# Three of 32 blocks, not four, are left out of the grouped expert pass

## The chip, the core and the metric

One Trainium2 chip, one of its cores. The time is that of one execution on the device in microseconds; a version's time is the median over its runs. The engines are TensorE (PE: matmuls, with weight loads beside them), VectorE (DVE), ScalarE (ACT), GpSimd (POOL) and SyncE (SP). Each works off its own queue of instructions in order. SP, ACT and POOL also issue transfers (DMA): SP and ACT plain ones, POOL here the indirect ones, whose row numbers come from a table on the chip. Everything is in fp32.

## The reference

Two layers on an image batch x of shape (4, 256, 64, 64). The first is a 3x3 neighbourhood attention behind a group normalisation; the second works on the 4 x 4096 tokens of 256 channels and ends with a mixture of 8 experts, of which each token uses 2:

```python
x = x + conv_attn(_gn(x))                  # 3x3 local attention, Wq, Wk, Wv, Wo
t = _to_tokens(x)                          # (4, 4096, 256)
t = t + windowed_gate(_ln_t(t))            # tanh projection, sigmoid gate, sums over 64 tokens
t = t + moe(_ln_t(t))
x = _from_tokens(t, x)

def moe(tokens):
    tokens = layer-normed t
    rw, re = top_k(softmax(tokens @ router_w.T), 2)    # rw scaled to sum 1
    out = tokens
    for e in range(8):
        h = gelu(tokens @ w1[e] + b1[e], approximate=False)
        out = out + combine[:, e:e+1] * (h @ w2[e] + b2[e])
    return out
```

## The kernel before

The 16384 tokens are worked in 32 blocks (`NB`) of 512 (`TB`), 8 blocks an image. For a block the functions `produce`, `attend`, `tail` and `ranks` run as generators, interleaved by the main loop (L1482): in turn g the block g is in `attend`, g - 1 in `tail`, g - 2 in `ranks`, g + 1 in `produce`. A scheduler then sets each engine's order from the program order and its own estimates.

*Tokens to experts.* `tail` ends with a block's normed tokens in `tok` (256 channels, 8 weights, 8 words with the place to which a result belongs). `ranks` counts, for each of the 1024 choices of a block, the row in the expert's region of the HBM array `rows_in`, and `give` (L1001) scatters the block with 8 indirect transfers on POOL, 128 rows each, one for each of 4 tiles and 2 choices. They wait in the list `waiting` and are let out a few at a time.

*Groups and slots.* Blocks are put in groups. When a group's last block is counted, a small plan is made on DVE (L1041 to L1112): how many full units of 256 rows (`UP`) each expert has by now, and so which expert and which rows each *slot* of the group has. A slot is 256 rows of one expert. A group of two blocks has 8 slots, one of one block 4; the first group has 7 fewer, so that there are always enough full units. `experts` runs a slot in stages: `fetch` (SP, L1171), `matrix` (ACT copies the expert's first matrix, L1188), `pixels` (PE transposes L1195, ACT copy L1199), `hidden` (PE L1207, ACT Gelu L1213), `output` (PE L1225, DVE L1229 and L1230) and `add` (L1244): two indirect transfers on POOL that add the results to `out`. The adds of one slot wait for those of the slot before to land, since two slots can hold one token's two choices. `follow` (L1466) says how many slots are due at each point of the main loop: between a limit `most`, which keeps them behind the groups' plans, and a straight line `wanted`, which ends 11, 7 and 3 slots before the last at turns NB, NB + 1 and NB + 2.

*Blocks apart.* The last four blocks (28 to 31, from `NS` on) are in no group. Their rows, with what is left of the groups' rows below a full unit (at most `LEFT` = 21 pieces), are worked at the end by `halves`, in `HALVES` = 2 * 4 * 512 / 128 + 21 = 53 *halves* of 128 rows: fetch (L1319), ACT copy of the matrix (L1331), transposes (L1334), products (L1344, Gelu L1350, L1360), DVE (L1364 to L1372). A half's result is scattered to `sums_a` by POOL (L1373), one row for each token and choice, so nothing has to be added there. The 21 left-over pieces are also added to `out` by L1390 for tokens of earlier blocks, each behind the add before. Each half gives a credit of 1, each such add, and each of the last three slots' adds, costs 2; what is owed at the last half is let out then.

*The end.* The tokens of the blocks apart stay in SBUF: `held` (L875) of blocks 28 and 29 in the pool `xsp`, those of 30 and 31 in their own tile `x1`. `together` (L1421) loads both choices' sums of a block from `sums_a` in two transfers of 512 KB, one on SP and one on ACT, adds them on DVE (L1448) and stores the block. The tiles for these loads take the place of other tiles: blocks 28 and 29 of the pool `xpp`, block 30 of the pool `w2p` (tag "wx"), block 31 of the pool `w3p` (tag "xl_tok"), whose three buffers the left-over pieces use before, four in each.

The lines that set groups and slots:

```python
NS = NB - 4
GROUPS = (*[2] * 13, *[1] * 2)
slots_of = [2 * n * TB // UP for n in GROUPS]
slots_of[0] -= E - 1
HALVES = 2 * (NB - NS) * TB // P + LEFT
```

They give 8 x 13 - 7 + 4 x 2 = 105 slots.

Of the kernel before, what the change touches and what calls it, by code (L numbers as in the profile page):

```python
# [46 lines left out]
FP = mybir.dt.float32  # L47
# [5 lines left out]
P = 128  # L53
# [9 lines left out]
def hybrid_block_kernel(ctx: ExitStack, tc: tile.TileContext, ins: dict, out: bass.AP):  # L63
    nc = tc.nc
    x = ins["x"]
    B, C, FW, _ = x.shape
# [4 lines left out]
    NT = TB // P  # L71
    NBI = HW // TB
    NB = B * NBI
    E = ins["w1b"].shape[0]
# [15 lines left out]
    FETCH = 2  # L90
    I32, U32 = mybir.dt.int32, mybir.dt.uint32
    ENG = mybir.EngineType
    NS = NB - 4
    GROUPS = (*[2] * 13, *[1] * 2)
    assert sum(GROUPS) == NS
    first_of = [sum(GROUPS[:k]) for k in range(len(GROUPS))]
    where = [(k, j) for k, n in enumerate((*GROUPS, NB - NS)) for j in range(n)]
    APART = len(GROUPS)

    U = 2  # L100
    UP = U * P
    slots_of = [2 * n * TB // UP for n in GROUPS]
    slots_of[0] -= E - 1
    assert slots_of[0] > 0
    first_slot = [sum(slots_of[:k]) for k in range(len(GROUPS) + 1)]
    LEFT = U * (E - 1) + E - 1
    HALVES = 2 * (NB - NS) * TB // P + LEFT
    SLOTS = max(*slots_of, HALVES)
# [3 lines left out]
    OWN = SPARE + HALVES * P  # L112
    ROOM_S = 2 * (NB - NS) * TB

# [9 lines left out]
    w2p = ctx.enter_context(tc.tile_pool(name="w2p", bufs=2))  # L124
# [137 lines left out]
    for d in range(2):  # L262
# [4 lines left out]
        part = near[:, d].rearrange("p a b -> p (a b)")  # L267
# [10 lines left out]
    for n in range(2):  # L278
        t = const.tile([P, NG, HALF], FP, tag=f"pe_{n}", name=f"pe_{n}")
# [41 lines left out]
    def iota(name, shape, pattern, base=0, by_partition=0):  # L321
        t = const.tile(shape, FP, tag=name, name=name)
        nc.gpsimd.iota(
            t, pattern=pattern, base=base, channel_multiplier=by_partition,
            allow_small_or_imprecise_dtypes=True,
        )
        return t
# [5 lines left out]
    place_a = iota(  # L333
        "place_a", [P, NB - NS, NT], [[2 * TB, NB - NS], [2 * P, NT]], base=OWN, by_partition=2
    )
# [84 lines left out]
    both = range(NC)  # L420
# [326 lines left out]
    def store(g, t, first=0):  # L747
        at = g * TB + first * P
        inst = nc.sync.dma_start(
            out[at : at + t.shape[1] * P, :].rearrange("(t p) c -> p t c", p=P), t  # L750
        ).ins
        tc.declare_no_dep(inst, group="adds", reason="sums of other blocks' rows")
        tc.add_to_no_dep_group("stores", inst)
        stored.append(inst)

    def tail(g):
# [18 lines left out]
        for pair in range(0, NT, 2):  # L775
            ps = ps_a.tile([P, 2, A + E], FP, tag="a", name=f"psp_{g}_{pair}")
            for u in range(2):
                t = pair + u
# [5 lines left out]
            for u in range(2):  # L784
                t = pair + u
# [13 lines left out]
        wx = w2p.tile([P, NT, C + 1 + E], FP, tag="wx", name=f"wx_{g}")  # L799
# [50 lines left out]
        for pair in range(0, NT, 2):  # L850
            ps = ps_a.tile([P, 2, C], FP, tag="a", name=f"psw_{g}_{pair}")
            window(ps, (slice(None), slice(pair, pair + 2), slice(0, C)))
            for u in range(2):
                t = pair + u
# [16 lines left out]
        if g < RAMP:  # L871
            scales()
        sent = t2
        if NS <= g < NS + 2:
            sent = xsp.tile([P, NC, TB], FP, tag="xs", name=f"held_{g}")  # L875
            sent = sent.rearrange("p c n -> p (c n)").rearrange("p (t c) -> p t c", t=NT)
        at = tc.cur_priority
# [543 lines left out]
    def together():  # L1421

        part = NT // 2
        for g in range(NS, NB):
            sums_of = None
            for n in range(0, NT, part):
                if g == NB - 1:
                    both = w3p.tile([P, NT, RW], FP, tag="xl_tok", name=f"both_{g}_{n}")
                    both = both.rearrange("p t r -> p (t r)")[:, 0 : 2 * part * C]
                    both = both.rearrange("p (t k c) -> p t k c", k=2, c=C)  # L1430
                elif g == NB - 2:
                    both = w2p.tile([P, NT, C + 1 + E], FP, tag="wx", name=f"both_{g}_{n}")
                    both = both.rearrange("p t r -> p (t r)")[:, 0 : 2 * part * C]
                    both = both.rearrange("p (t k c) -> p t k c", k=2, c=C)
                else:
                    if n == 0:
                        sums_of = xpp.tile([P, NT, 2, C], FP, tag="xp", name=f"both_{g}")
                    both = sums_of[:, n : n + part]
                first = OWN + 2 * ((g - NS) * TB + n * P)
                (nc.scalar if n else nc.sync).dma_start(  # L1440
                    both,
                    sums_a[first : first + 2 * part * P, :].rearrange(
                        "(t p k) c -> p t k c", p=P, k=2
                    ),
                )
                own = held[g][:, n : n + part]
                for k in range(2):
                    nc.vector.tensor_add(own, own, both[:, :, k, :])  # L1448
                store(g, own, n)
# [32 lines left out]
    for g in range(NB + 2):  # L1482
        for n in range(*stats_at[g]):
            channel_stats(n)
        if g + 1 < NB:
            for n in range(*stats_at[g + 1]):
                load_xs(n)
        gens = [attend(g), ranks(g - 2), tail(g - 1), produce(g + 1)]
        if g + 3 < NB and (g + 3) % NBI == 0:
            gens.append(image_norm((g + 3) // NBI))  # L1490
        if g == 2:
            load_experts()
        n = 0
        while gens:
            for gen in list(gens):
                if next(gen, gens) is gens:
                    gens.remove(gen)
                    continue
                n += 1
                follow(g + min(n / STEPS.get(g, 27), 0.999))  # L1500
# [6 lines left out]
    for rest in (stream, units):  # L1507
        for _ in rest:
            pass
    together()  # L1510


# [56 lines left out]
```

## Time and profile before

| | us |
|---|---|
| median of 9 runs | 1217.36 |
| lowest, highest | 1214.28, 1220.08 |
| the profiled execution | 1214.2 |
| its span in the profile | 1212.5 |

| lines | work | count | busy us | mean ns |
|---|---|---|---|---|
| L1207, L1225, L1195 (PE) | a slot's products and transposes | 840, 840, 420 | 204.9, 213.2, 65.2 | 385, 385, 278 |
| L1244 (POOL) | adds of slots to `out` | 210 | 335.3 | 1596 |
| L1001 (POOL) | scatters of tokens to `rows_in` | 256 | 256.3 | 1001 |
| L1229, L1230 (DVE) | a slot's bias and weight | 210, 210 | 87.5, 76.6 | 417, 365 |
| L1373 (POOL) | scatters of halves to `sums_a` | 53 | | 957 to 1087 |
| L1390 (POOL) | adds of left-over pieces to `out` | 21 | | 1589 to 1619 |

A row of the groups' table names line, engine and operation, with the sum of the durations and their mean. A matmul in fp32 shows as two records, so 840 records of L1207 are 4 matmuls in each of 105 slots. The order of the stages is seen from the first and last starts: L1244 runs from 188.9 to 1083.7 us, L1001 from 84.7 to 1037.6, L1373 from 1066.2 to 1189.9, L1390 from 1088.3 to 1182.9, and the additions of `together` from 1197.5 on. The clock granted to PE over the span is 0.976 of full speed.

### The profile page before, as it was taken

How to read it: one execution, taken by the hardware profiler on the slowest of the kernel's cores; microseconds unless marked ns; L12 is line 12 of the kernel's file. 1: busy time of each engine (PE TensorE's matmuls, PEld its weight loads, DVE VectorE, ACT ScalarE, POOL GpSimd, SP SyncE). 2: the span in 40 equal slices, each digit the busy share in tenths (PEclk: the TensorE clock that was granted, in tenths of full speed). 3: DMA queues.
4: the chain of work that ended last, by engine and by line, in shares of the span. 5: the costliest groups of instructions: out<-in, count | busy, mean ns of one | idle time of the engine just before them, and what ended most of it. 6: DMA issues, size and time to landing. Idle time of an engine off the chain costs nothing. (4 is left out here: it accounts for less than half of the span.)

```text
span 1212.5 us, 29026 instructions
## 1 busy us (share of the span) xinstructions
PE 1108.1 (91%) x8762; PEld 791.5 (65%) x8762; DVE 916.0 (76%) x4632; ACT 856.2 (71%) x1752; POOL 703.9 (58%) x642
## 2 busy tenths in 40 slices
PE   5989889999999999999999999999999999868890
PEld 4545456677776667766677766766776677757780
DVE  4588878888888888887888887888878888324444
ACT  1466769788888788777787787877787766436660
POOL 3114226566664666576665756566565768577772
PEclk9999999999999999999999999999999999979996
DMA  9895547776768677778786767667665446745556
GB/s 283 267 308 177 175 138 238 209 173 169 186 177 173 160 222 178 187 200 215 164 166 166 192 171 179 168 172 173 141 171 128 101 103 135 177 88 122 144 124 238
DMA packets 136145, 214.00 MB, mean 176 GB/s; under 512 B 16368, under 2 KB 102400, under 8 KB 131768
## 3 DMA queue, kind: packets, MB, share of 16 engines
q1 hardware_dynamic: 86264, 137.00, 37.1%
q0 software_dynamic: 48352, 73.05, 30.3%
q10 hardware_dynamic: 1376, 2.10, 0.5%
q8 instruction: 73, 1.20, 0.4%
q14 instruction: 80, 0.66, 0.2%
HBM read 120.78 MB, written 91.31 MB: 175 GB/s over the span
## 5 line engine op out<-in xcount | busy, mean ns | idle before, releaser
L1244 POOL DMA_INDIRECT out<-sx x210 | 335.3, 1596 | 202.8 <-issue 32.2
L1001 POOL DMA_INDIRECT rows_in<-tok,rows x256 | 256.3, 1001 | 195.4 <-issue 72.5
L1225 PE MATMUL psy<-w,h 128*128 x840 | 213.2, 385 | 1.2 <-DVE qbb L525 0.7
L1207 PE MATMUL psh<-xc,w1s 128*128 128x256 f32 x840 | 204.9, 385 | 0.3 <-ACT h L1213 0.3
L1225 PEld LDWEIGHTS psy<-w,h 128*128 128x128 f32 x840 | 152.7, 190 | 51.6 <-issue 24.9
L1207 PEld LDWEIGHTS psh<-xc,w1s 128*128 128x128 f32 x840 | 152.5, 191 | 35.3 <-issue 10.0
L576 PE MATMUL psq<-x,qks 128*128 128x512 f32 x256 | 125.5, 612 | 1.8 <-ACT qks L497 1.8
L734 PE MATMUL pso<-mixT,vo 128*128 128x512 f32 x256 | 123.5, 605 | 0.0
L1229 DVE TENSOR_TENSOR sx<-psy,b2b 128x256 f32<-128x256 f32 x210 | 87.5, 417 | 44.8 <-PE psy L1225 36.6
L1213 ACT ACTIVATE h<-psh,w1s 128x256 f32<-128x256 f32 x210 | 88.2, 471 | 31.1 <-PE psh L1207 30.2
L1199 ACT COPY xc<-ptx 128x512 f32<-128x512 f32 x105 | 61.2, 583 | 25.4 <-PE ptx L1195 24.9
L1230 DVE TENSOR_SCALAR sx<-sx 128x256 f32<-128x256 f32 x210 | 76.6, 365 | 2.0
L893 ACT ACTIVATE x<-x,scale 128x256 f32<-128x256 f32 x120 | 63.2, 591 | 18.8 <-DVE scale L867 15.4
L1213 ACT ACT_TABLE_LOAD x59 | 75.7, 1283 | 0.8
L584 ACT ACTIVATE q<-psq,qbb,irc 128x512 f32<-128x512 f32 x64 | 50.0, 781 | 34.5 <-PE psq L576 28.1
L1195 PE MATMUL ptx<-ident,sx 128*128 128x128 f32 x420 | 65.2, 278 | 6.8 <-DMA sx<-rows_in 6.8
L1195 PEld LDWEIGHTS ptx<-ident,sx 128*128 128x128 f32 x420 | 50.6, 144 | 31.4 <-issue 16.3
L780 PE MATMUL psp<-wpr,x1c 128*128 128x136 f32 x512 | 70.2, 282 | 0.5 <-DVE ispread L473 0.5
L576 PEld LDWEIGHTS psq<-x,qks 128*128 128x128 f32 x256 | 46.2, 195 | 35.5 <-issue 34.5
L780 PEld LDWEIGHTS psp<-wpr,x1c 128*128 128x128 f32 x512 | 65.5, 190 | 4.7 <-issue 2.1
L734 PEld LDWEIGHTS pso<-mixT,vo 128*128 128x128 f32 x256 | 45.5, 190 | 34.3 <-issue 30.1
L832 PE MATMUL psw<-wl,bandl 128*64 128x512 f32 x128 | 67.0, 635 | 0.0
(277 smaller groups left out, 2498.6 us busy)
## 6 DMA issues: line engine op xcount, KB each, us to landing
xp<-in_xp SPq DMA_DIRECT2D x32, 1024.0 KB
sx<-rows_in SPq DMA_DIRECT2D x105, 272.0 KB
x<-in_x SPq DMA_DIRECT2D x32, 660.0 KB
xs<-in_xs SPq DMA_DIRECT2D x32, 512.0 KB
out<-x SPq DMA_DIRECT2D x28, 512.0 KB
sxa<-rows_in SPq DMA_DIRECT2D x32, 136.0 KB
rows_in<-tok,rows POOLq DMA_INDIRECT x256
out<-sx POOLq DMA_INDIRECT x210
```

The costliest lines, as they stand in the source:

```text
L576: inst = nc.tensor.matmul(ps.rearrange("p (r w) -> p r w", w=W), qks[:, ci, co * P : (co + 1) * P], t[:, ci, 1 : TH + 1, 1 : W + 1], start ...
L734: nc.tensor.matmul(ps, vo[:, ci, co * P : (co + 1) * P], mixT[:, ci, :], start=(ci == 0), stop=(ci == NC - 1),)
L780: nc.tensor.matmul(ps[:, u, :], xc[:, ci, t * P : (t + 1) * P], wpr[:, ci, :], start=(ci == 0), stop=(ci == NC - 1),)
L832: one = nc.tensor.matmul(to[0:WIN], bandl, wl[part], start=True, stop=True)
L1001: return nc.gpsimd.indirect_dma_start(out=rows_in[:, :], out_offset=bass.IndirectOffsetOnAxis(ap=rows[:, c, t : t + 1], axis=0), in_=tok[: ...
L1195: nc.tensor.transpose(pt[:, c, t * P : (t + 1) * P], xs[:, t, c * P : (c + 1) * P], ident)
L1207: nc.tensor.matmul(ps[:, f, :], w1s[:, o : o + P], xc[:, ci, :], start=(ci == 0), stop=(ci == NC - 1),)
L1213: inst = nc.scalar.activation(h[:, f, :], ps[:, f, :], AF.Gelu, bias=w1s[:, F1 + f : F1 + f + 1])
L1225: nc.tensor.matmul(ps, h[:, f, t * P : (t + 1) * P], w2[:, e, f, :], start=(f == 0), stop=(f == NC - 1),)
L1229: nc.vector.tensor_add(ys[:, t, :], ps, b2b[:, e, :])
L1230: nc.vector.tensor_scalar_mul(ys[:, t, :], ys[:, t, :], xs[:, t, bass.ds(e + C, 1)])
L1244: inst = nc.gpsimd.indirect_dma_start(out=out, out_offset=bass.IndirectOffsetOnAxis(ap=xs[:, t, C + E : C + E + 1].bitcast(U32), axis=0), ...
```

## The change

Block 28 becomes a group of its own, the sixteenth, with four slots; three blocks stay apart. So there are 109 slots and 45 halves where there were 105 and 53. Only block 29 is held in `xsp`, blocks 30 and 31 in their own tiles; block 28 is stored by `tail` and gets its experts' results by adds to `out`. `together` loads the sums of blocks 29 and 30 into the pool `xpp`, those of block 31 into `w3p` as before; the branch for `w2p` goes.

```diff
-    NS = NB - 4
-    GROUPS = (*[2] * 13, *[1] * 2)
+    NS = NB - 3
+    GROUPS = (*[2] * 13, *[1] * 3)
...
-        if NS <= g < NS + 2:
+        if g == NS:
             sent = xsp.tile([P, NC, TB], FP, tag="xs", name=f"held_{g}")
...
                 if g == NB - 1:
                     both = w3p.tile([P, NT, RW], FP, tag="xl_tok", name=f"both_{g}_{n}")
-                    both = both.rearrange("p t r -> p (t r)")[:, 0 : 2 * part * C]
-                    both = both.rearrange("p (t k c) -> p t k c", k=2, c=C)
-                elif g == NB - 2:
-                    both = w2p.tile([P, NT, C + 1 + E], FP, tag="wx", name=f"both_{g}_{n}")
                     both = both.rearrange("p t r -> p (t r)")[:, 0 : 2 * part * C]
                     both = both.rearrange("p (t k c) -> p t k c", k=2, c=C)
                 else:
```

## The prediction

> **What bounds the kernel now.** I read the page first, then busy time by stretch of the span, then the timelines of TensorE (PE), GpSimd (POOL) and VectorE (DVE). A row of the stretch table has its length, then busy time and number of instructions of PE, weight load, DVE, ACT and POOL, then PE's granted clock, DMA share and GB/s.
>
> ```profile
> PE 1108.1 (91%) x8762; PEld 791.5 (65%) x8762; DVE 916.0 (76%) x4632; ACT 856.2 (71%) x1752; POOL 703.9 (58%) x642
> ...
> 250.00:417.00 167.00, 165.91 (x1333) 119.33 (x1331) 140.60 (x725) 138.03 (x260) 100.57 (x85) 1.00 0.72 171
> 417.20:956.10 538.90, 533.88 (x4319) 374.87 (x4317) 451.19 (x2359) 422.42 (x826) 346.38 (x285) 1.00 0.71 173
> 956.00:1043.00 87.00, 79.48 (x437) 64.05 (x434) 71.49 (x336) 53.20 (x103) 62.26 (x50) 0.98 0.57 127
> 1043.00:1066.00 23.00, 15.29 (x96) 13.65 (x96) 4.00 (x14) 11.20 (x29) 9.30 (x6) 0.86 0.78 171
> 1066.00:1192.00 126.00, 99.52 (x646) 85.87 (x646) 49.99 (x166) 70.47 (x181) 94.92 (x80) 0.95 0.51 118
> 1192.00:1212.50 20.50, 0.00 (x0) 0.00 (x0) 9.99 (x16) 0.00 (x0) 0.00 (x0) 0.50 0.86 307
> ```
>
> The reader is to see three regimes. From 250 to 956 PE is busy over 99% at full clock: it sets the time. From 1066 to 1192 (the 128-row halves) PE has 26 us to spare. From 1192 on only transfers and 16 additions are left. The busy sum of the first regime might hide gaps, so I looked at starts:
>
> ```profile
> 625.98 1.89 PE L1207 MATMUL psh<-xc,w1s 128*128 128x256 f32 x8
> 627.71 1.03 PE L1225 MATMUL psy<-w,h 128*128 x4
> 628.66 0.65 PE L618 MATMUL pss<-x,q 128*32 128x60 f32 x32
> 629.24 1.98 PE L734 MATMUL pso<-mixT,vo 128*128 128x512 f32 x4
> 631.06 1.03 PE L1225 MATMUL psy<-w,h 128*128 x4
> 631.93 0.60 PE L1195 MATMUL ptx<-ident,sx 128*128 128x128 f32 x4
> 632.36 1.89 PE L1207 MATMUL psh<-xc,w1s 128*128 128x256 f32 x8
> ```
>
> Each group starts where the one before lets it in, with no idle time noted. From start to next start, a slot's parts here take 0.95 + 0.87 (L1225), 0.43 (L1195) and 1.73 (L1207). In the second regime look at POOL:
>
> ```profile
> 1178.42 1.59 POOL L1390 DMA_INDIRECT out<-sxl,token  x1 [0.44 <-issue]
> 1180.32 0.98 POOL L1373 DMA_INDIRECT sums_a<-sxa,to  x1 [0.30 <-DVE sxa L1371]
> 1181.60 0.96 POOL L1373 DMA_INDIRECT sums_a<-sxa,to  x1 [0.30 <-issue]
> 1182.86 1.60 POOL L1390 DMA_INDIRECT out<-sxl,token  x1 [0.30 <-issue]
> ...
> 1189.91 0.96 POOL L1373 DMA_INDIRECT sums_a<-sxa,to  x1 [0.30 <-issue]
> ```
>
> Between two of its instructions lie 0.30 us whatever is named as releaser, so a scatter (L1373) takes 1.28 and an add (L1390, L1244) 1.90. From the first scatter at 1066.17 to the end of the last at 1190.87 are 124.7 us: 53 x 1.28 + 21 x 1.90 + 6 x 1.90 (the three slots' L1244 still in it) = 119.1, and 5.6 in which an add waits for the one before it to land. POOL's queue sets this stage; its 75% busy doesn't show that, the gaps do.
>
> **The change part by part.** *Amount of work.* `slots_of` gives a one-block group 4 slots of 256 rows; `HALVES` falls from 53 to 45. In the order in which the two builds lay out PE's instructions, both are alike up to block 13; then blocks 14 to 30 hold 65 slots where before they held 61, four a block up to block 20. What follows the last dispatch on POOL is alike (seven pairs of L1244, the last three with scatters between, then scatters and L1390) except for its length.
>
> *Four slots more in the PE-bound stretch.* Over 250 to 956 the mean from start to next start is 1.78 (L1207), 0.92 twice (L1225) and 0.47 (L1195): 4.09 a slot, 4 x 4.09 = **+16.4**. Bounds: the densest quarter of the same rows gives 1.73 + 2 x 0.86 + 0.44 = 3.89, +15.6; the page's busy sums, (213.2 + 204.9 + 65.2) / 105 = 4.60, +18.4, which count overlaps twice. I take the starts.
>
> *Eight halves fewer in the POOL-bound stretch.* 8 x 1.28 = 10.2. The built order ends in "scatter, add, add" instead of "add, five scatters", so two adds drop out from before the last scatter, 3.8, with two of 20 waits, 0.6: **-14.6**. Lower bound 10.2, if the adds must be waited for after all; upper bound the stage's pace, 8 x 124.7 / 53 = 18.8.
>
> *The end.* `together` handles three blocks:
>
> ```profile
> 1197.52 2.50 DVE L1448 TENSOR_TENSOR held<-held,both 128x512 f32<-128x512 f32 x4 [8.44 <-DMA both<-sums_a]
> 1200.74 2.50 DVE L1448 TENSOR_TENSOR held<-held,both 128x512 f32<-128x512 f32 x4 [0.72 <-DMA both<-sums_a]
> 1203.40 5.11 DVE L1448 TENSOR_TENSOR x<-x,both 128x512 f32<-128x512 f32 x8 [0.17 <-DMA both<-sums_a]
> ```
>
> Loads of 1 MB a block arrive 3.22 and 2.66 apart, the last at 1206.02 by the chain: 2.62. One block less saves 2.6. A new wait takes some back: block 31's second load reuses the rows of leftovers 16 to 19, and add 19 now comes after the last scatter. Nothing is behind that load on ACT's queue; the additions and store of the last half block wait for it. With T the start of the last scatter (1189.91 before), add 18 starts at T - 1.9, and adds here follow each other by 4.45 to 5.5, so 19 starts at T + 2.6 to 3.6 and its issue takes 1.6. After a pair of L1244 the next starts 3.85 to 4.3 us later (1042.30 to 1046.45 less the 0.30). So the load goes out at T + 8.0 to 9.5 instead of T + 4. The first load took 5.1 from issue to use; this one would be there by T + 13.1 to 14.6, where without the wait it is T + 13.5. I take 0.5 back: **-2.1**, bounds 0 and -3.2.
> The Trainium skill, "DMA: Bandwidth & Descriptors", section "Anatomy of one DMA — SWDGE (gpsimd) path", puts a transfer at about 2.0 us fixed plus bytes over 436 GB/s. The trace's 3.85 to 4.3 is longer than the 2.3 this gives for 128 KB, and its 2.62 to 3.22 a block longer than the page's 2.4; by the page the new wait costs nothing, the block saves only 2.4, and the sum below would be -0.6.
>
> *Costed at nothing.* Eight more L1244 on POOL (15.2 us) lie before 956, where POOL is 64% busy; without that cover they cost the 15.2. Group 15's plan (L1041 to L1112, some 15 DVE instructions of 0.15 to 0.21) and the adds of psy (0.42 + 0.37, twice a slot) lie beside PE; DVE has 88 us free there. Uncovered: 3 and 6. Block 28's store moves before 956, into a DMA share of 0.71, and x1 of block 30 reuses its buffer some 60 us later; four fetches on SP's queue go the same way, and group 15's first one needs block 28's rows dispatched: at the old pace that ends at 964.2, and the fetch four from the last goes out at 1006.98. ACT's queue gets four slots' copies and Gelus and, by the built order, 128 table loads for 118, the ten in blocks 14 to 21:
>
> ```profile
> L1213 ACT ACT_TABLE_LOAD x59 | 75.7, 1283 | 0.8
> ```
>
> That is 8.6 + 10 x 1.28 = 21.4 us on an engine with 116 free from 417 to 956. Blocks before 417 already carry six loads each and four slots: ACT is 83% busy there and PE still 99%. So nothing, upper bound 12.8.
>
> *Sum.* 16.4 - 14.6 - 2.1 = -0.3. The profiled execution took 1214.2 (span 1212.5 and 1.7 around it), 3.2 below the median, just under the lowest run; -0.3 on the median is **1217.1**.
>
> **The rivals.** *Faster:* the halves shed their full pace, 18.8, and the end a first-pair share, 3.2: 16.4 - 18.8 - 3.2 = -5.6, 1211.8. For it: POOL idles 30 of 126 us. Against: those are the 0.30 gaps, and the 21 adds stay.
> *Slower:* ACT's ten table loads reach PE. Place: blocks 14 to 21, where PE's Gelu results come later and L1225 waits. If half of them do, -0.3 + 6.4 = +6.1, 1223.5; it decides from 2.7 / 12.8 = 21% on. For it: "PE psh" ends most waits of L1213 (30.2 us), so the pair runs closely coupled. Against: the blocks before 417.
> *A wait in place of the one removed:* add 19 lands late because the block loads keep the DMA at 0.86. If it took 8 us instead of 4.3, the last load would be in use at T + 17.8 on the mean, 4.3 late; the third term becomes +1.7 and the time 1220.9.
> *The change not doing what it says* I exclude: slots, halves and blocks are counted in the built order.
>
> **How the numbers follow.** About 0.2%, 2.4 us, is what a measurement can tell from no change. Level (the sum) 0.46: 0.05 faster, 0.35 within, 0.06 slower; its own range, each term half way to its bounds, is 1214 to 1221. Faster rival 0.21: 0.20 and 0.01 within. ACT rival 0.26: 0.25 slower, 0.01 within. Late add 0.07: 0.01, 0.01, 0.05. Together 0.26, 0.38, 0.36. All low ends give 16.4 - 18.8 - 3.2 with 15.6 for the slots: -6.4; all high ends without ACT 18.4 - 10.2: +8.2. I cut both a little: 1211.5 to 1224.
>
> **What would show it.** The time of block 31's first transposes (L688, 956.1 before) moves to about 972; first scatter to last shrinks from 124.7 to about 110; last scatter to the end from 22.6 to about 20.5. If the first moves by over 20 with table loads ahead of Gelu as the releaser, the ACT rival holds; if POOL shows waits over 0.3 in the halves, the second term was mis-sized.

## The result, and the profile after

The changed kernel takes 1242.7 us (median of 19 runs, 1235.29 to 1252.23) where the kernel before took 1215.1 beside it (62 runs, 1206.34 to 1223.44): ratio 1.0222, 95% interval 1.0205 to 1.0239. It is slower by about 27 us; 1217.1 was predicted, with 1224 as the upper end. Executions that fell into a slower state of the chip are left out of the medians, ratios and intervals given here. A ratio is not exactly the quotient of the two medians beside it. The profiled execution has a span of 1245.8 us against 1212.5; it took 1247.55 us, 4.9 more than the median, so the two profiles lie further apart (33 us) than the two medians (27.6).

First the page's busy times, then busy time by stretch (length, then busy time and instructions of PE, weight load, DVE, ACT and POOL, granted clock, DMA share, GB/s). The stretches are cut at events: first transposes of block 14 and of block 31, first scatter of a half, end of the last one. In the kernel before these lie at 417.3, 956.1, 1066.2 and 1190.9 us. The second row is a piece of the first.

```profile
PE 1114.0 (89%) x8730; PEld 797.1 (64%) x8730; DVE 914.1 (73%) x4640; ACT 863.3 (69%) x1746; POOL 706.8 (57%) x642
```

```profile
420.10:1000.50 580.40, 552.48 (x4399) 390.68 (x4398) 459.81 (x2393) 443.43 (x855) 357.66 (x294) 0.98 0.68 166
570.00:600.00 30.00, 6.27 (x45) 3.65 (x46) 6.35 (x23) 3.36 (x6) 8.99 (x8) 0.60 0.53 140
1000.50:1111.80 111.30, 97.08 (x534) 80.11 (x532) 74.28 (x352) 63.14 (x130) 70.67 (x55) 0.93 0.59 132
1111.80:1225.20 113.40, 84.12 (x532) 73.45 (x532) 42.73 (x142) 57.48 (x148) 84.04 (x70) 0.91 0.49 107
1225.20:1245.80 20.60, 0.00 (x0) 0.00 (x0) 7.49 (x12) 0.00 (x0) 3.14 (x3) 0.50 0.80 252
```

PE's total work is nearly what it was (1114.0 against 1108.1 us). The loss lies in the first stretch: 580.4 us where it was 538.9, with 27.9 us in which PE does nothing, where there were 5.0. The halves are shorter, 113.4 against 124.7. The second row holds most of the idle time: in 30 us PE works 6.3, and the other engines are idle for two thirds of it or more. The starts of the blocks agree: block 18 is 57.5 us long where it was 31.9, no other one from block 14 on is over 35.

Three timelines tell what happened there (start, duration, engine, line, operation, in brackets the idle time before it and what ended that): PE's, VectorE's and SyncE's.

```profile
567.97 1.97 PE L1207 MATMUL psh<-xc,w1s 128*128 128x256 f32 x8
593.73 3.75 PE L734 MATMUL pso<-mixT,vo 128*128 128x512 f32 x4 [23.79 <-DVE row L980]
```

```profile
565.85 0.36 DVE L977 TENSOR_TENSOR so_far<-so_far,psk 128x8 f32<-128x8 f32 x2
592.06 0.69 DVE L179 BATCH_NORM_STATS2 stats<-xs 128x6 f32<-128x512 f32 x1 [25.85 <-DMA xs<-in_xs]
```

```profile
555.16 0.42 SPq L165 DMA_DIRECT2D xs<-in_xs  x1
572.09 6.59 SPq L1171 DMA_DIRECT2D sx<-rows_in  x3
578.78 0.41 SPq L152 DMA_DIRECT2D xp<-in_xp  x1
579.29 0.39 SPq L749 DMA_DIRECT2D out<-x  x1
579.77 0.46 SPq L165 DMA_DIRECT2D xs<-in_xs  x1
```

Read from the bottom. The load of `xs` (L165, block 31's channels for the group statistics) is issued at 579.77. It stands behind a store and another load, and these behind three fetches (L1171), of which the first is that of the first slot of group 7 and waited 15.8 us, within 0.1 of the longest such wait in the stretch. What it waited for is the group's last scatter into `rows_in` on POOL's queue, the 128th of L1001:

```profile
569.32 0.99 POOL L1001 DMA_INDIRECT rows_in<-tok,rows  x1 [0.30 <-issue]
```

VectorE came to the statistic of that load (L179) at 566.2 and stood until 592.06: 13.6 us until the load was issued, and 12.3 us from there until it had landed. Everything behind it on VectorE's queue, among it `row` (L980) and what PE's next product needs, stood too. In the built order the changed kernel has the statistics of block 31 ahead of those of block 30, some 190 VectorE instructions earlier than in sequence; the kernel before has them in sequence, and there block 31's load goes out 47 us ahead of its statistic:

```profile
567.99 0.41 SPq L165 DMA_DIRECT2D xs<-in_xs  x1
```

```profile
615.24 0.68 DVE L179 BATCH_NORM_STATS2 stats<-xs 128x6 f32<-128x512 f32 x1
```

So two things met: a statistic that was placed early, and its load behind a fetch that waits. Why the scheduler places them so was not followed.

Such waits are common in the changed kernel. Summed over 400 to 1010 us (total, number, longest), the fetches on SyncE's queue waited for scatters and for adds to land, before and then after:

```profile
SPq L1171 <- DMA rows_in<-tok,rows: 27.9, 4, 12.3
SPq L1171 <- DMA out<-sx: 377.7, 78, 14.7
```

```profile
SPq L1171 <- DMA rows_in<-tok,rows: 94.8, 9, 15.9
SPq L1171 <- DMA out<-sx: 270.9, 60, 11.8
```

The waits for scatters grew; those for adds, the larger part, shrank by more: the two together are 365.7 us, where they were 405.6. The sum doesn't make the loss: what stands behind one fetch, and when somebody needs it, does.

The end, on POOL's queue and then VectorE's:

```profile
1199.77 1.60 POOL L1390 DMA_INDIRECT out<-sxl,token  x1 [3.03 <-issue]
...
1224.24 0.98 POOL L1373 DMA_INDIRECT sums_a<-sxa,to  x1 [0.30 <-issue]
1226.49 1.57 POOL L1390 DMA_INDIRECT out<-sxl,token  x1 [1.27 <-DMA out<-sxl,token]
1235.43 1.55 POOL L1390 DMA_INDIRECT out<-sxl,token  x1 [7.37 <-DMA out<-sxl,token]
```

```profile
1232.50 2.50 DVE L1444 TENSOR_TENSOR held<-held,both 128x512 f32<-128x512 f32 x4 [13.10 <-DMA both<-sums_a]
1235.75 3.10 DVE L1444 TENSOR_TENSOR x<-x,both 128x512 f32<-128x512 f32 x5 [0.76 <-DMA both<-sums_a]
1240.81 1.90 DVE L1444 TENSOR_TENSOR x<-x,both 128x512 f32<-128x512 f32 x3 [1.96 <-DMA both<-sums_a]
```

Two left-over adds come after the last scatter. The first of them starts at 1226.49 and has landed when the second starts, at 1235.43: with the block loads running it takes nearly 9 us. The last half block's sums wait for it; VectorE waits 1.96 us for these.

### The profile page after: what moved, and what is told of

It reads as the page before. It is cut to its first block, busy times and chain, and to the rows that moved or that the text cites. A ratio compares the mean times of both kernels' runs of the same rounds, so it can differ in the third digit from the quotient of the medians.

```text
span 1245.8 us, 28921 instructions
## 1 busy us (share of the span) xinstructions
PE 1114.0 (89%) x8730; PEld 797.1 (64%) x8730; DVE 914.1 (73%) x4640; ACT 863.3 (69%) x1746; POOL 706.8 (57%) x642
## 5 line engine op out<-in xcount | busy, mean ns | idle before, releaser
L1244 POOL DMA_INDIRECT out<-sx x218 | 346.7, 1590 | 238.6 <-issue 33.2
L1001 POOL DMA_INDIRECT rows_in<-tok,rows x256 | 255.3, 997 | 198.3 <-issue 75.2
L1225 PE MATMUL psy<-w,h 128*128 x872 | 219.8, 384 | 1.6 <-issue 0.9
L1207 PE MATMUL psh<-xc,w1s 128*128 128x256 f32 x872 | 214.0, 388 | 0.2
L1225 PEld LDWEIGHTS psy<-w,h 128*128 128x128 f32 x872 | 159.1, 190 | 56.4 <-issue 26.3
L1207 PEld LDWEIGHTS psh<-xc,w1s 128*128 128x128 f32 x872 | 158.6, 191 | 40.2 <-issue 6.4
L734 PE MATMUL pso<-mixT,vo 128*128 128x512 f32 x256 | 128.8, 627 | 23.8 <-DVE row L980 23.8
L1229 DVE TENSOR_TENSOR sx<-psy,b2b 128x256 f32<-128x256 f32 x218 | 91.3, 419 | 48.2 <-PE psy L1225 40.2
L1213 ACT ACTIVATE h<-psh,w1s 128x256 f32<-128x256 f32 x218 | 91.6, 471 | 24.3 <-PE psh L1207 23.4
L893 ACT ACTIVATE x<-x,scale 128x256 f32<-128x256 f32 x124 | 65.3, 590 | 20.6 <-DVE scale L867 16.1
L1199 ACT COPY xc<-ptx 128x512 f32<-128x512 f32 x109 | 63.6, 584 | 19.3 <-PE ptx L1195 18.8
L823 ACT COPY wl<-wx 64x795 f32<-64x795 f32 x32 | 27.2, 851 | 67.3 <-DVE wx L811 67.1
L1195 PEld LDWEIGHTS ptx<-ident,sx 128*128 128x128 f32 x436 | 53.3, 145 | 28.7 <-issue 14.9
L1188 ACT COPY w1s<-w1b 128x514 f32 x109 | 68.0, 630 | 1.5
```

The lines of the kernel that those rows point to most:

```text
L734: nc.tensor.matmul(ps, vo[:, ci, co * P : (co + 1) * P], mixT[:, ci, :], start=(ci == 0), stop=(ci == NC - 1),)
L1001: return nc.gpsimd.indirect_dma_start(out=rows_in[:, :], out_offset=bass.IndirectOffsetOnAxis(ap=rows[:, c, t : t + 1], axis=0), in_=tok[: ...
L1188: nc.scalar.copy(w1s, w1b[:, e, :])
L1195: nc.tensor.transpose(pt[:, c, t * P : (t + 1) * P], xs[:, t, c * P : (c + 1) * P], ident)
L1207: nc.tensor.matmul(ps[:, f, :], w1s[:, o : o + P], xc[:, ci, :], start=(ci == 0), stop=(ci == NC - 1),)
L1213: inst = nc.scalar.activation(h[:, f, :], ps[:, f, :], AF.Gelu, bias=w1s[:, F1 + f : F1 + f + 1])
```

## The experiments

Kernels of one batch ran on one chip and are compared with the kernel before of the same batch, which took 1270.46, 1219.44, 1255.20, 1220.65 and 1273.07 us in the five batches; times of different batches are not compared. Batches 2 and 4 alone have the changed kernel itself. The first theory: one stall, made by the order of the statistics; take it away and little is left. Its rival: the four slots' own price. Later a second one came up, that SyncE's queue delays stores as well.

### The changed kernel again (batches 2 and 4)

> The changed kernel once more, on one chip with the next three. Theory (a statistic of block 31 ahead of its blocked load): one wait of DVE at L179 of 20 us or more around block 18, PE idle as long, 1.5 to 2.5% above the kernel before. If the wait is an accident of one execution or one chip, it is missing here and the ratio is within 0.5% of 1.

> The changed kernel as it is, for the other three of this call. Both theories: one idle time of VectorE of 20 to 26 us for block 31's load in block 18, and 1.5 to 2.3% slower than before; the lower end if the granted clock is low on this chip, because then the other stages are longer and the stall (a transfer that waits for scatters) is not.

1.0221 [1.0179, 1.0264] and 1.0212 [1.0176, 1.0248], 25.6 and 24.6 us over the kernel before. VectorE's one wait for block 31's load was 23.2 and 24.1 us. The stall is in every profile of this kernel.

The kernel before was also profiled in batch 2:

> The kernel before on the same chip, for its trace: no wait of over 5 us at L179, about 125 us from the first to the last scatter of the halves, 22 to 23 us from there to the end.

1218.63 us, span 1216.8; blocks 14 to 31 took 540.0 us, its fetches waited 32.5 us for scatters in 4 waits, VectorE had no wait at L179 in this stretch, first scatter to last took 126.1, and from the start of the last scatter to the end it was 22.9.

### The statistics in sequence (batches 1, 2 and 4)

```diff
-    xs_of, stats = {}, {}
+    xs_of, stats, last_stat = {}, {}, []
...
+                if last_stat:
+                    after(inst, last_stat[-1], "statistics in turn")
+                last_stat.append(inst)
```

> The changed kernel with one more ordering edge: the statistics (L179) of a block stay behind those of the block before, so block 31's no longer stand ahead of block 30's in DVE's queue. SP's order stays as it is. Theory (one statistic placed ahead of its load, which waits in SP's queue behind a slot's fetch): the 25.9 us wait of DVE and PE's 23.8 us go, median 1217 to 1221 against 1242.7. Rival 1 (four slots a block make the fetches wait for the dispatch and the whole front is late): stays above 1235. Rival 2 (ten more table loads or a dearer slot): stays above 1235.

> The edge between statistics once more, beside the changed kernel on the same chip. Theory: 1.5 to 2.2% below the changed kernel, within 0.5% of the kernel before. Rivals 1 and 2 (fetches behind the dispatch, dearer slots): within 0.5% of the changed kernel.

> The statistics in turn. Both theories: no idle time for that load, 10 to 20 us (0.9 to 1.6%) less than a_third of this call. What is left against before: up to 1.0%.

1.0008 [0.9971, 1.0046], 1.0105 [1.0068, 1.0142] and 1.0099 [1.0067, 1.0132]. Against the changed kernel of the same batch it is 13.8 and 12.9 us faster. The wait of L179 is gone in all three. The built order of PE, SyncE and POOL is the same with the edge as without it, and ScalarE's nearly so: the order on VectorE made the stall. But a stall of some 23 us went and only 13 came back, 1.1% and not the 1.5% or more that was expected; some 12 us over the kernel before, 1%, are left in batches 2 and 4, where at most 0.5% was expected in batch 2. Where they are shows in block 21, which is 40.6 us long in the third of these profiles where it was 33.4 in the changed kernel. PE's, ACT's and SyncE's timelines there (the edit moves the lines by 3):

```profile
667.28 0.59 PE L472 MATMUL gm<-imean,gavg 128*128 128x2 f32 x2 [5.67 <-ACT x L771]
```

```profile
666.65 1.07 ACT L771 COPY x<-ptx 128x512 f32<-128x512 f32 x2 [6.96 <-DMA out<-x]
```

```profile
649.76 5.85 SPq L1174 DMA_DIRECT2D sx<-rows_in  x3
655.71 0.41 SPq L152 DMA_DIRECT2D xp<-in_xp  x1
656.21 0.39 SPq L752 DMA_DIRECT2D out<-x  x1
```

The same queue once more: the store of a block stands behind fetches that wait, ACT can't write the next block's rows into the buffer `x1` until the store has landed, and PE waits for ACT. In all, ACT waited 10.5 us for stores in this stretch, and PE 6.8 us for ACT's copy behind them; the kernel before shows no such wait. In the changed kernel of the same batch it was 7.6 and 4.0 us, which fits stores that landed during the stall there.

### The loads on ACT's queue (batch 1)

```diff
-        nc.sync.dma_start(
+        (nc.scalar if g >= 16 else nc.sync).dma_start(
```

(in `load_xs`, without the edge.)

> The changed kernel with the loads for the statistics of blocks 16 to 31 issued from ACT instead of SP. DVE's order keeps block 31's statistics ahead of block 30's, and SP's fetch still waits for the dispatch. Theory: the load is out before DVE asks for it, no wait of over 5 us at L179, median 1217 to 1223. If the early place in DVE's queue alone were enough, without the blocked SP queue: a wait of 10 us or more remains and the median is above 1228. Rivals 1 and 2: above 1235.

1.0063 [1.002, 1.0106]. The statistics of block 31 are still ahead of block 30's, but the load no longer stands behind fetches, and the long wait of L179 is gone (1.1 us in the stretch is left). So taking away either half of the cause, order or queue, is enough to undo the stall. Against the edge on the statistics in the same batch it is 8 us slower. Why isn't known: this build also has ten table loads fewer on ACT than the changed kernel (118, as the kernel before) and another order in many places.

### A buffer of its own at the end (batches 1 and 2)

With the edge, and for the last half block's sums the pool that the change gave up:

```diff
-                    both = w3p.tile([P, NT, RW], FP, tag="xl_tok", name=f"both_{g}_{n}")
+                    if n:
+                        both = w2p.tile([P, NT, C + 1 + E], FP, tag="wx", name=f"both_{g}_{n}")
+                    else:
+                        both = w3p.tile([P, NT, RW], FP, tag="xl_tok", name=f"both_{g}_{n}")
```

> As e1, and the last block's second load gets a buffer of its own (pool of wx) instead of the rows of leftovers 16 to 19. Theory (that load waits for add 19 to land, 8.7 us after its issue): last scatter to the end falls from 21.6 us to 19.5 to 20.3, median 1 to 2 below e1. Rival (the loads are bound by the DMA rate anyway): no change of last scatter to end.

> Edge and a buffer of its own for the last half block, beside e1 on the same chip. Theory: 0.1 to 0.2% below e1, the last scatter to the end 1 to 2 us shorter. Rival (the loads at the end are bound by the DMA rate): the same as e1.

0.9992 [0.995, 1.0035] and 1.0100 [1.0062, 1.0138]: 2.3 and 2.0 us less than the edge alone, within what the intervals leave open, but the profiles show the mechanism: from the start of the last scatter to the end 20.1 us in batch 2 where the edge alone has 20.9 and the kernel before 22.9, and the wait ahead of the last additions is gone (1.17 us with the edge alone).

### A lower price of the adds (batch 1)

As before, and the credit that an add costs goes from 2 to 1.8, so that no add is left behind the last scatter.

```diff
-                    owed.append((2.0, sum_))
+                    owed.append((1.8, sum_))
...
-                owed.append((2.0, lambda: add(m, x_)))
+                owed.append((1.8, lambda: add(m, x_)))
```

> As e4, and an owed add costs 1.8 halves of credit, not 2, so that the last two adds don't stand behind the last scatter. If POOL's queue bounds the halves, two more adds (3.8 us) come before the last scatter and the time from first to last scatter grows from 113 to 115 to 118, while the end no longer has adds beside it (less than 1 us gained): median 1 to 4 above e4. If PE or DVE bound the halves, nothing changes.

1.0045 [1.0006, 1.0083]. First scatter to last becomes 117.8 us where the kernel with the buffer alone has 112.0, last scatter to the end 19.2 where it has 20.7: 5.9 paid for 1.5. In these two profiles adds pulled in front of the last scatter cost more there than behind it; the time is 8 us longer, more than the 1 to 4 that were expected, and the rest of it lies ahead of the halves.

### The stores on ACT's queue (batches 3, 4 and 5)

With the edge and the buffer, the blocks' stores are issued by ScalarE:

```diff
-        inst = nc.sync.dma_start(
+        inst = (nc.scalar if RAMP <= g < NS else nc.sync).dma_start(
```

> As e4 (edge between statistics, buffer of its own at the end), and the stores of blocks 7 to 28 go out from ACT's queue, not from SP's, so that they no longer stand behind a fetch that waits for the dispatch. Theory A (what is left of the loss, 10 to 12 us, is SP's queue: late stores hold x1's buffer, ACT's copy L771 and then PE): ACT's waits for out<-x go, 4 to 8 us below e4, within 0.6% of the kernel before. Theory B (a slot simply costs PE 6 us, not 4.1): same as e4, 1.0% above the kernel before.

> The statistics in turn, a buffer of its own at the end, and the blocks' stores issued by ScalarE instead of behind the fetches. Theory P (the slots' own price): within 0.2% of e1_third. Theory Q (late stores): 0.5 to 1.0% faster than e1_third, so between 0.5% faster than before and 0.3% slower; ScalarE shows no wait for a store of a block.

> The changed kernel with the statistics in turn, the buffer at the end, and the same stores on ScalarE. Theory Q (late stores behind fetches): between 0.7% faster than before and 0.2% slower. Theory P (slots' own price): 0.5 to 1.2% slower than before.

0.9944 [0.9914, 0.9974], 0.9994 [0.9972, 1.0017] and 0.9925 [0.9878, 0.9972]. In batch 4, where all stand side by side: changed kernel 1245.25, with the edge 1232.38, with edge, buffer and stores 1219.38, kernel before 1220.65. The buffer's part is about 2, so the stores' is about 11. ACT has no wait for a store left, although the fetches wait for scatters as long as ever (95.8 us in 9 waits in batch 4): the stores no longer stand behind them. The built order of VectorE and POOL is the same as with the edge alone. So the slots' own price isn't the rest of the loss: what was left at the edge went when the stores (and the 2 us of the buffer) moved. Not all of the 11 us is seen at the late stores, though: in the profiles of batch 4 the stretch from block 14 to 31 became 5.3 us shorter. The edge's profile was the slowest of its six executions; just ahead of block 14 its granted clock was 0.92 (380 to 424.5 us), where the changed kernel had 1.00.

### The fetches one slot later (batches 3 and 4)

The changed kernel without the edge, with `most` (the limit on the slots) one slot lower:

```diff
-    most = [(at, max(0, n - FETCH - 1)) for at, n in zip(
+    most = [(at, max(0, n - FETCH - 2)) for at, n in zip(
```

> The changed kernel with the limit on slots one slot further back (n - FETCH - 2), nothing else: a group's first fetch stands later in SP's queue. Theory A: SP's waits for rows_in fall from 91 to 95 us between 400 and 1010 to below 50, the wait of 20 us at block 18 goes, 1.5 to 2.3% below the changed kernel, 0 to 0.6% above the kernel before. Theory B: only the wait at block 18 can go, 1.0% above the kernel before.

> The changed kernel without the edge, with each slot's fetch placed one slot later. Theory Q: the waits of SyncE's fetches for scatters fall from some 90 to 60 to 70 us, block 31's load goes out before VectorE comes to its statistics, and the time is 1.0 to 2.0% less than a_third. Theory P: the stall alone goes (as in e1_third) and the time stays within 0.3% of e1_third.

1.003 [0.9998, 1.0062] and 1.0059 [1.0031, 1.0087]; in batch 4 17.4 us less than the changed kernel. The fetches' waits for scatters fall to 69.6 us (longest 12.5), in batch 3 to 67.2, where below 50 was expected. VectorE has no wait for block 31's load. But that doesn't show that a later fetch saves it: in the built order of this kernel the statistics of block 31 stand behind those of block 30 again, so the stall had lost its other half too. A store is still late: block 21 is 46.2 us long, with a wait of ACT for `out` of 9.3 us. What the distance between a group's last scatter and its first fetch is worth by itself stays open.

### The kernel before with denser slots (batch 3)

```diff
-    wanted = [(begins[1], 1), *((NB + n, first_slot[-1] - m) for n, m in ((0, 11), (1, 7), (2, 3)))]
+    wanted = [(begins[1], 1), (20.35, 54), *((NB + n, first_slot[-1] - m) for n, m in ((0, 11), (1, 7), (2, 3)))]
```

> The kernel before (four blocks apart, 105 slots) with the changed kernel's pace: four slots a block up to block 20, then fewer; the amount of work is unchanged. Theory A (the pace at the limit makes the loss, not the four slots): SP's waits for rows_in between 400 and 1010 rise from 28 to 33 us to 70 or more, 0.3 to 1.0% above the kernel before. Theory B (the slots' own cost): no change, within 0.2%.

0.9993 [0.9959, 1.0027]. The slots follow the changed kernel's pace up to block 20, the fetches wait 49.0 us for scatters, and nothing is lost. A miss for the theory that the pace alone brings the loss, but a weak one: the waits didn't reach the 70 us that it asked for, and in batch 1, which was slow as well (1270.46 us), the edge alone had lost nothing either.

### The kernel before with its stores on ACT's queue (batches 3 and 5)

The diff of the stores alone, on the kernel before.

> The kernel before with the same stores on ACT's queue: the control for e6. Theory A: hardly a store is late there, within 0.3% of the kernel before. If stores on ACT are better or worse by themselves, it shows here.

> The kernel of before with the blocks' stores issued by ScalarE. If the 1.6% of its first timing was real: 1.0 to 2.0% slower than before, with blocks of some 42 us in the stretch from block 14 to 31 whose PE idle time ends on something behind a store on ScalarE's queue. If it was chance: within 0.3%, all blocks 30 to 36 us.

1.016 [1.0099, 1.0221] and 1.0174 [1.0106, 1.0241], so the first was not chance, and the control missed. Moving the stores is no gain by itself; in the kernel before it is a loss. The cause stays open. Blocks 18 and 20 are 42 us long in the first of these profiles, block 20 is 40 in the second, with a wait of VectorE ahead of L625 of 9.0 and 11.8 us for which the trace names no instruction of this core. PE's idle time from block 14 to 31 is 31.9 and 35.5 us, where the kernel before has 5.6 in batch 2; 9.5 and 13.8 of it end on VectorE's L789 (0.9 before). The built order of VectorE is the same as before, ScalarE's isn't, beyond the stores themselves. The version with all three edits shows a part of the same price: 4.8 us of PE's idle time end on that line in batch 4 (0.2 with the edge alone).

## Why the prediction was wrong, point by point

The parts of the span in five profiles (us), cut as above. "All three" is edge, buffer and stores.

| | before, 2 | changed, on record | changed, 4 | edge, 4 | all three, 4 | all three less before |
|---|---|---|---|---|---|---|
| to block 14 | 419.2 | 420.1 | 416.0 | 424.5 | 421.4 | +2.2 |
| blocks 14 to 31 | 540.0 | 580.4 | 586.1 | 564.3 | 559.0 | +19.0 |
| to the first scatter | 109.6 | 111.3 | 111.8 | 112.3 | 109.7 | +0.1 |
| first to last scatter | 126.1 | 113.4 | 111.2 | 114.3 | 109.7 | -16.4 |
| to the end | 21.9 | 20.6 | 20.4 | 20.1 | 19.3 | -2.6 |

The headings name the batch; the last column crosses batches 2 and 4, whose kernels before are 1.2 us apart.

*Amount of work.* Right: 109 slots, 45 halves, no more on POOL than was counted.

*Four slots more, +16.4 (15.6 to 18.4).* Nearly right. The stretch grew by 41.5 us on record; without the 23.8 us of PE's stall 17.7 are left, and 19.0 where no store is late either (17.3 of PE's busy time and 1.7 of idle time). That is 4.4 to 4.75 a slot: the page's busy sums (4.60) were the better row, and the starts (4.09) the worse one.

*Eight halves fewer, -14.6 (10.2 to 18.8).* Right in size: -11.3 on record, -14.9 between the two profiles of batch 2 (111.3 against 126.1), -16.4 above. The eight scatters and two adds account for 14.0 (10.2 and 3.8), as summed. The 0.6 for two waits was the loose part: POOL's time beyond the 0.30 between two instructions adds up to 6.1 us before and 8.6 on record (the longest waits 3.03 and 2.56), but to 7.4 and 6.6 in batch 2. That is the smaller saving of the one execution. Waits over 0.3 were named as the sign that the term is mis-sized; the kernel before has them as well, up to 1.37, so they alone tell nothing.

*The end, -2.1 (0 to -3.2).* The block's share was right: last scatter to the end falls by 2.8 where the last half block has a buffer of its own (20.1 against 22.9 in batch 2). The new wait was under-priced: add 19 took 8.7 us to land, not 4.3, and -1.0 was left on record. That is the mechanism of the *wait in place of the one removed*, whose premise of 8 us held; its price of 3.8 was too high: the last additions start 16.6 us after the start of the last scatter, not 17.8. With and without the wait, 20.9 and 20.1, it is 0.8, and 1.1 by the difference to the prediction. The 2.4 us a block given there beside the sum is worked out from a rate for transfers that POOL issues; the block loads go out on SyncE and ScalarE, and the sum doesn't rest on it.

*Costed at nothing.* This is the step that failed. It said that "four fetches on SP's queue go the same way", and asked only when the last group's fetches go out. But the slots come earlier everywhere from block 14 on, so fetches of the groups in the middle run up against their groups' scatters (94.8 us of waits for 27.9), and every load and store queued behind them on SyncE waits with them. One such wait of 15.8 us, with a statistic placed early, held VectorE for 25.85 us and PE for 23.8. The prediction looked at what the change adds to that queue, not at what stands behind a fetch there. It also compared PE's and ACT's built order and not VectorE's, where the statistics of block 31 had moved ahead. Taking each away gave back 13 us for the order and some 11 for the stores; the rest of this step held, block 28's plan, adds and store cost nothing that the profiles show.

*ACT's ten table loads reach PE.* Fell. It forecast the right side by a wrong mechanism. In blocks 14 to 31 of the changed kernel the groups of L1213 and L1225 read:

```profile
L1213 ACT ACT_TABLE_LOAD x42 | 53.9, 1283 | 0.5
```

```profile
L1225 PE MATMUL psy<-w,h 128*128 x524 | 133.7, 385 | 1.1 <-issue 0.5 <-DVE den L693 0.3 <-DVE tst_f L647 0.3
```

Six loads more than before (36) ahead of Gelu, and the idle time of the product that would wait for them is 1.1 us in all, none of it ended by ACT. The version with all three edits has even 130 table loads in its whole trace, for 118 before, and is level with the kernel before in batch 4. The *faster* rival fell too on record. With the stall and the late stores gone the sum of the terms is within 0.3% of the kernel before in batch 4, where the prediction had put it, but partly by luck: slots 2.6 us dearer than predicted, and 2.2 us ahead of block 14 that nobody had costed, stand against halves and end that saved 1.8 and 0.5 more. In batches 3 and 5 that version is faster than the prediction by over 0.5%.

*What would show it.* Block 31's transposes moved by 44.4 us, not 16; "by over 20 with table loads ahead of Gelu" was the only test given for that, and the releaser named here, a load behind SyncE's queue, was not on the list.

The version with all three edits beats the kernel before in batches 3 and 5, by 0.56 and 0.75%, and equals it in batch 4, where it is 2.1% faster than the changed kernel.

## What to carry to other kernels

SyncE's queue handed the wait of one fetch, 15.8 us, to all transfers behind it: when a change makes a transfer wait longer, list the loads and stores that stand behind it and ask who waits for those, even if the change adds nothing to them. Compare the built order on every engine, not only on the one that sets the time; one instruction placed 190 places early cost 13 us net. And when a stall is taken away, expect back less than its length: here part of it seems to have been time in which late stores landed.

## What was not expected of the hardware

The kernel before took 1270 and 1219 us in batches 1 and 2, on the same chip; the cause stays open. The profiles of the edge in these two have nearly the same granted clock (0.962 and 0.973); in the longer one most blocks are longer, by up to 5 us, PE's busy time from block 14 to 31 is 572.1 us for 555.1, and ACT and VectorE show waits for which no instruction of the core is named (17.5 us on the four longest lines from 400 to 1010 us), in the shorter one none. The comparison differs as well: the edge alone is 1.05% behind the kernel before in one and level in the other. In the stall PE's granted clock was 0.60 on the mean over 30 us, and the first product behind it took 3.75 us for four matmuls that took 1.98 in the kernel before.
